# Full-array and tiled products of a step gathered into one row each, in the first pass of an attention kernel

## The chip, the cores and the metric

The kernel runs on one core of a Trainium2 chip. The core has a matrix engine (TensorE, PE in the profile; its weight loads are PEld), VectorE (DVE), ScalarE (ACT) and GpSimd (POOL), and sixteen DMA engines that move data between HBM and the on-chip memory. The engines run side by side, each through its own queue in order, and wait for each other by semaphores. The metric is the device time of one execution in microseconds, the median of several runs. Before the change it is 4040.75 us (3 runs, 4040.39 to 4041.5).

## The reference: what is computed

The input x is 8 images of 256 channels and 64 x 64 pixels, all in fp32. Two layers follow each other. Cut to what matters:

```python
# layer 0: attention of every pixel to 256 reduced keys, 8 heads of 32 channels
xr = conv(x, w_sr, stride 4)                    # 16 x 16 = 256 tokens
xr = layernorm over channels(xr) * norm_g + norm_b
q  = w_q @ x;  k, v = split(w_kv @ xr)
out = softmax(q k^T * 32**-0.5) v               # for each head
x  = x + gamma_s * (w_out @ out)
# layer 1: linear attention over two scales
qkv = w_qkv @ x                                 # 768 channels
agg = grouped 1x1 (w_pw) of depthwise 5x5 (w_dw) of qkv
... linear attention with relu, projection w_proj, batch norm, added to x
```

The change concerns layer 0 and the product qkv of layer 1, which the kernel computes together.

## The kernel before

The kernel has three passes (`first_pass`, `second_pass`, `third_pass`), and a general version that is run only where the softmax sums of the first pass leave a safe range. Only `first_pass` is changed. It does layer 0 and the qkv product.

The work is cut into steps. `order` lists them: for each image b, each of 8 strips s of 512 pixels, each half c of the heads (4 heads, 128 channels) and each half kc of the 256 keys. That makes 32 steps an image and 256 in all; n is the number of a step, and odd n are those with kc = 1. The loop runs 16 steps further to finish what is behind.

What a step asks of TensorE comes in two kinds. Products of the **full array** have 128 rows and 128 columns of weights: `queries` (q, L759), the qkv products (L885), the output products of `added` (o, L840), the stride convolution (sr, L687) and the small products of `keys_values`. Products in **tiles** use 32 rows or 32 columns of the array, so that four heads run at once: `scores` (sc, L774, four row tiles), `valued` (av, L793, four column tiles) and `counted` (den, L809, four column tiles). A matmul in fp32 shows as two records in the trace.

The chain of a step: `scores` puts four heads' scores into four of five PSUM banks (tag "mm", which the full-array products share); ScalarE turns them into exponentials e (L780). One step later, as m = n - 1, `valued` multiplies them with the values into av. At the end of an odd step `joined` (L804) lets GpSimd add the exponentials of both halves of the keys, in place, in the tiles of the even step; so these adds wait for the av that still reads these tiles. `counted` in the next even step multiplies the sums with ones, which gives the softmax denominators den. `normed` copies av (ScalarE) and divides: VectorE transposes den (L819), takes reciprocals (L820), transposes back (L822) and multiplies (L824). The result att waits two steps for `added`.

The qkv product of a pair of strips is made from 21 full-array products (`qkv`, seven for each of three pairs). They are spread over the seven steps after a pair of strips is done: `todo[n]` holds the products of step n, 2, 3, 4, 1, 4, 3 and 4 of them for n mod 8 = 3, 4, 5, 6, 7, 0 and 1, none for n mod 8 = 2. Output products come in the steps with n mod 4 = 2. For the next image, `keys_values` runs ahead in the steps with n mod 32 from 12 to 25: the stride convolution first, small products after it.

The loop body sets the order on each engine. In an odd step TensorE's row is: scores, the qkv products, valued. In an even step: scores, valued, the qkv products, queries, counted, then output products (n mod 4 = 2) and keys work where there is any. Tile, the framework, may depart from this: it orders each engine's instructions when the kernel is built, by when it believes their inputs ready, and by the written order among those that are ready. `tc.keep_in_program_order` ties one instruction behind everything written before it on its engine.

Of the kernel before, what the change touches and what calls it, by code (L numbers as in the profile page):

```python
# [574 lines left out]
def first_pass(ctx: ExitStack, tc: tile.TileContext, a, fine, planes, x2d, kd, vd, wtd):  # L575
    nc = tc.nc
# [23 lines left out]
    def load_x(b):  # L600
        x_tiles[b] = xpools[b % 2].tile([P, 2, HW], F32, tag="x", name=f"x_{b}")
        for s in range(NG):
            load_strip(b, s)
# [42 lines left out]
    def border(b):  # L646
        v = vd[b].rearrange("n y x e -> y x n e")
        src = nil.rearrange("p (n e) -> p n e", n=8)
        for i in (0, NB2 + 1):
            nc.sync.dma_start(v[i], src)  # L650
            nc.sync.dma_start(v[1 : NB2 + 1, i], src[:NB2])
# [104 lines left out]
    def queries(b, s, c):  # L756
        ps = bank(f"q_{b}_{s}_{c}")
        for ci in range(2):
            nc.tensor.matmul(  # L759
                ps,  # L760
                consts["wq"][:, ci, c * P : (c + 1) * P],
                x_tiles[b][:, ci, s * QB : (s + 1) * QB],
                start=(ci == 0),
                stop=(ci == 1),
            )
        qs = two.tile([P, QB], F32, tag="q", name=f"q_{b}_{s}_{c}")
        nc.scalar.copy(qs, ps)
        return qs

    def scores(b, s, c, kc, qs):  # L770
        scs = [bank(f"sc_{b}_{s}_{c}_{kc}_{h}") for h in range(4)]
        for h in range(4):
            rows = slice(h * D0, (h + 1) * D0)
            nc.tensor.matmul(  # L774
                scs[h], kks[b][rows, c, kc * P : (kc + 1) * P], qs[rows], start=True, stop=True
            )
        es = []
        for h in range(4):
            e = two.tile([P, QB], F32, tag="e", name=f"e_{b}_{s}_{c}_{kc}_{h}", bufs=E_BUFS)
            nc.scalar.activation(e, scs[h], AF.Exp, scale=D0**-0.5)  # L780
            es.append(e)
        return es
# [5 lines left out]
    def valued(b, s, c, kc, es):  # L788
        if kc == 0:
            sums["av"] = psum_early.tile([P, QB], F32, tag="av", name=f"av_{b}_{s}_{c}")  # L790
        for h in range(4):
            cols = slice(h * D0, (h + 1) * D0)
            nc.tensor.matmul(  # L793
                sums["av"][cols],
                vvs[b][:, kc, c * P + h * D0 : c * P + (h + 1) * D0],
                es[h],
                start=(kc == 0),
                stop=(kc == 1),
            )


    def joined(es0, es1):
        for h in range(4):
            nc.gpsimd.tensor_tensor(es0[h], es0[h], es1[h], ALU.add)  # L804

    def counted(b, s, c, es):
        sums["den"] = psum_early.tile([P, QB], F32, tag="den", name=f"den_{b}_{s}_{c}")
        for h in range(4):
            nc.tensor.matmul(sums["den"][h * D0 : (h + 1) * D0], ones_w, es[h], start=True, stop=True)  # L809

    def normed(b, s, c):
        av, den = sums["av"], sums["den"]
        i = 2 * ((b * NG + s) * 2 + c)
        att = rest.tile([P, QB], F32, tag="att", name=f"att_{b}_{s}_{c}", bufs=4)
        turn = rest.tile([P, NB, D0], F32, tag="rden", name=f"rden_{b}_{s}_{c}", bufs=1)
        one = two.tile([P, NB], F32, tag="one", name=f"one_{b}_{s}_{c}")
        nc.scalar.copy(att, av)

        nc.vector.transpose(turn.rearrange("p n d -> p (n d)"), den)  # L819
        nc.vector.reciprocal(one, turn[:, :, 0])  # L820
        r = rest.tile([P, NB, D0], F32, tag="rall", name=f"rall_{b}_{s}_{c}", bufs=1)
        nc.vector.transpose(r, one.unsqueeze(2).to_broadcast([P, NB, D0]))  # L822
        r = r.rearrange("p n d -> p (n d)")
        nc.vector.tensor_mul(att, att, r)  # L824

        def noted():
            for k, t in enumerate((turn[:, :, 0], one)):
                copy = two.tile([P, NB], F32, tag="copy", name=f"copy_{b}_{s}_{c}_{k}")
                tc.keep_in_program_order(
                    nc.scalar.activation(copy, t, AF.Copy, accum_out=seen[:, i + k : i + k + 1])  # L830
                )

        late.append(noted)
        return att

    def added(b, s, att, oc):
        xt, cols = x_tiles[b], slice(s * QB, (s + 1) * QB)
        ps = bank(f"o_{b}_{s}_{oc}")
        for c in range(2):
            nc.tensor.matmul(ps, consts["wout"][:, c, oc * P : (oc + 1) * P], att[c], start=(c == 0), stop=(c == 1))  # L840
        nc.vector.scalar_tensor_tensor(  # L841
            xt[:, oc, cols], ps, consts["gam"][:, 0:1], xt[:, oc, cols], ALU.mult, ALU.add
        )
        nc.sync.dma_start(x2d[b][oc * P : (oc + 1) * P, cols], xt[:, oc, cols])
# [5 lines left out]
    def differences(b, g):  # L850
        xt = x_tiles[b]
        x = xt[:, :, 2 * g * QB : 2 * (g + 1) * QB].rearrange("p c (h n) -> p c h n", h=2)
        b11, b12, b21, b22 = (x[:, c, h] for c in range(2) for h in range(2))
        t = halves.tile([P, 4, QB], F32, tag="differences", name=f"differences_{b}_{g}", bufs=1)
        t1, t2, t3, t4 = (t[:, i] for i in range(4))
        nc.vector.tensor_sub(t1, b12, b11)
        nc.vector.tensor_sub(t2, b22, t1)
        nc.gpsimd.tensor_tensor(t3, b22, b12, ALU.subtract)
        nc.vector.tensor_sub(t4, t2, b21)
        quarters[b, g] = b11, b21, b22, t1, t2, t3, t4  # L860
# [130 lines left out]
    order = [(b, s, c, kc) for b in range(B) for s in range(NG) for c in range(2) for kc in range(2)]  # L991
    q, es, att = {0: first}, {}, {}
    ahead = iter(())

    def qkv_lazy(b, g, pair):
        made = []

        def go(i):
            def run():
                if i == 0:  # L1000
                    made.extend(qkv(b, g, pair))
                made[i]()

            return run

        return [go(i) for i in range(7)]

    n_all = len(order)
    todo = {}
    for n in range(n_all + 16):  # L1010
        m = n - 1
        if n < n_all:
            b, s, c, kc = order[n]
            es[n] = scores(b, s, c, kc, q[n // 2])
        was, late[:] = list(late), []
        for f in was:
            f()


        if n % 2:  # L1020
            for f in todo.pop(n, ()):
                f()
        if 0 <= m < n_all:
            valued(*order[m], es[m])
        for f in todo.pop(n, ()):
            f()
        if n < n_all and kc == 0 and n + 2 < n_all:
            q.pop(n // 2 - 1, None)
            q[n // 2 + 1] = queries(*order[n + 2][:3])
        if 0 <= m < n_all and order[m][3] == 1:  # L1030
            counted(*order[m][:3], es.pop(m - 1))
            es.pop(m)
            att[order[m][:3]] = normed(*order[m][:3])
        if n < n_all and kc == 1:
            joined(es[n - 1], es[n])
        if n >= 6 and (n - 6) % 4 == 0 and (n - 6) // 4 < B * NG:
            b, s = (n - 6) // 4 // NG, (n - 6) // 4 % NG
            for oc in range(2):
                added(b, s, [att[b, s, 0], att[b, s, 1]], oc)
            if s % 2:  # L1040
                differences(b, s // 2)
                products = [p for pair in (1, 2, 0) for p in qkv_lazy(b, s // 2, pair)]
                for i, count in enumerate((2, 3, 4, 1, 4, 3, 4)):
                    todo[n + 1 + i] = products[:count]
                    products = products[count:]
        next(weights, None)
        if n < n_all:
            b, at = n // 32, n % 32
            if at == 2:
                border(b)  # L1050
            if b + 1 < B:
                if at == 10 and b > 0:
                    load_x(b + 1)
                if at == 12:
                    ahead = keys_values(b + 1)
                if 12 <= at < 20:
                    next(ahead)
                    next(ahead)
                elif at >= 20:
                    next(ahead, None)  # L1060
# [545 lines left out]
def kernel_body(ctx: ExitStack, tc: tile.TileContext, a, out):  # L1606
# [19 lines left out]
    wtd = [scratch(f"wt_{j}", [P, 16, 6 * P]) for j in range(4)]  # L1626

    first_pass(tc, a, fine, planes, x2d, kd, vd, wtd)
    second_pass(tc, a, planes, kd, vd, wtd, kvd, attd)
    third_pass(tc, a, planes, x2d, kvd, attd, out)  # L1630
# [118 lines left out]
```

## Time and profile before

The profile is one execution; its span is 4041.7 us. The first pass ends at about 2133 us, where the check of the softmax sums (L1070) runs.

| engine | busy us of 4041.7 | busy us of one image of the first pass (825 to 1082 us) |
|---|---|---|
| TensorE | 3954.6 (98%) | 256.2 of 257 |
| VectorE | 2250.5 (56%) | 141.5 |
| ScalarE | 1511.8 (37%) | 105.9 |
| GpSimd | 1275.2 (32%) | 93.2 |

| group in the first pass | count | mean ns of one |
|---|---|---|
| L774 sc, 32 rows, 512 columns streamed | 2048 | 642 |
| L793 av, 32 columns of weights, 512 streamed | 2048 | 610 |
| L809 den, the same form | 1024 | 605 |
| L759 q, full array, 512 streamed | 512 | 601 |
| L804 GpSimd add of two 128 x 512 tiles | 512 | 1315 |

A mean duration of a matmul holds its way through the array, so that records overlap; what a product costs is read from the distance between starts in the timeline. A line of the timeline gives the start and the length of a run of like instructions, in microseconds, with the idle time ahead of it and what ended that, in square brackets.

### The profile page before, as it was taken

The numbers are of one execution on the slowest core, as the hardware profiler recorded it, in microseconds if no ns is written. First come the engines' busy times: TensorE is split into PE (matmuls) and PEld (weight loads), VectorE is DVE, ScalarE is ACT, GpSimd is POOL, SyncE is SP. The second block draws the span as 40 slices with busy tenths as digits, with TensorE's granted clock in tenths as the row PEclk, the third lists the DMA queues.
The fourth block names the chain that finished last, engine by engine and source line by source line (L and its number), as shares of the span: only waits on it lengthen the run. The fifth ranks groups of instructions, "written<-read, shape, count | busy, mean of one in ns | idle before, by whom it ended". The sixth has DMA issues, their size and how long they took to land. (4 is left out here: it accounts for less than half of the span.)

```text
span 4041.7 us, 70298 instructions
## 1 busy us (share of the span) xinstructions
PE 3954.6 (98%) x27074; PEld 2260.2 (56%) x27074; DVE 2250.5 (56%) x3752; ACT 1511.8 (37%) x3473; POOL 1275.2 (32%) x1394
## 2 busy tenths in 40 slices
PE   8999999999999999999997999999999998999999
PEld 4333433434334343343335888888888886556555
DVE  2576465564655645555664566666666664444443
ACT  2334344343443434434432222222222223555444
POOL 2334233343343433424433344444444440000000
PEclk9999999999999999999998999999999998999999
DMA  7655444435344353434548878778778756767674
GB/s 236 186 172 144 143 105 145 103 98 155 93 141 112 96 157 93 134 105 107 137 111 237 247 223 235 221 219 236 222 219 233 208 167 173 229 197 235 196 235 138
DMA packets 569897, 691.37 MB, mean 171 GB/s; under 512 B 60112, under 2 KB 429264, under 8 KB 565328
## 3 DMA queue, kind: packets, MB, share of 16 engines
q1 hardware_dynamic: 569552, 686.78, 60.0%
q8 instruction: 215, 3.52, 0.4%
q14 instruction: 130, 1.06, 0.1%
HBM read 412.54 MB, written 274.10 MB: 170 GB/s over the span
## 5 line engine op out<-in xcount | busy, mean ns | idle before, releaser
L804 POOL TENSOR_TENSOR e<-e,e 128x512 f32<-128x512 f32 x512 | 656.2, 1315 | 867.0 <-PE av L793 867.0
L780 ACT ACTIVATE e<-sc 128x512 f32<-128x512 f32 x1024 | 530.6, 602 | 939.1 <-PE sc L774 939.1
L1205 PE MATMUL cv<-w,c 128*128 128x128 f32 x3072 | 386.5, 280 | 9.7 <-POOL c L1149 9.7
L1205 PEld LDWEIGHTS cv<-w,c 128*128 128x128 f32 x3072 | 361.1, 193 | 40.6 <-issue 30.3
L774 PE MATMUL sc<-q,kk 32*128 32x512 f32 x2048 | 312.9, 642 | 11.7 <-DVE x L841 5.3
L1572 DVE TENSOR_TENSOR y<-z,xs 128x256 f32<-128x256 f32 x256 | 142.6, 644 | 316.3 <-ACT z L1563 291.0
L1247 PE MATMUL sums<-vq,r 128*32 128x288 f32 x4096 | 308.3, 414 | 0.0
L885 PE MATMUL qkv<-differences,combined 128*128 128x512 f32 x576 | 306.4, 623 | 1.9 <-DVE whole L901 1.0
L819 DVE STREAM_TRANSPOSE rden<-den 128x512 f32<-128x512 f32 x128 | 91.7, 716 | 369.6 <-PE den L809 369.5
L793 PE MATMUL av<-e,vv 128*32 128x512 f32 x2048 | 275.2, 610 | 0.0
L1221 ACT ACTIVATE r<-s 128x512 f32<-128x512 f32 x256 | 160.5, 627 | 293.5 <-DVE s L1220 289.9
L1209 PE MATMUL cv<-c,w 128*128 128x128 f32 x2048 | 253.4, 277 | 0.0
L1554 PE MATMUL p<-att,wproj 128*128 128x512 f32 x512 | 249.9, 610 | 1.9 <-ACT att L1537 1.9
L1563 ACT ACTIVATE z<-p,bn 128x256 f32<-128x256 f32 x256 | 133.8, 578 | 314.8 <-PE p L1554 241.3
L687 PE MATMUL sr<-x,wsr 128*128 128x256 f32 x1024 | 238.3, 387 | 7.7 <-DMA wsr<-in_w_sr_dram 7.7
L759 PE MATMUL q<-x,wq 128*128 128x512 f32 x512 | 245.3, 601 | 0.2 <-DVE whole L901 0.2
L1554 PE MATMUL p<-agg,wproj 128*128 128x512 f32 x512 | 242.3, 596 | 0.0
L1212 ACT COPY both<-cv 128x512 f32<-128x512 f32 x128 | 75.0, 586 | 444.3 <-PE cv L1205 386.8
L1209 PEld LDWEIGHTS cv<-c,w 128*128 128x128 f32 x2048 | 239.7, 192 | 0.0
L840 PE MATMUL o<-att,wout 128*128 128x512 f32 x512 | 237.7, 605 | 0.0
L687 PEld LDWEIGHTS sr<-x,wsr 128*128 128x128 f32 x1024 | 193.2, 192 | 73.8 <-issue 40.8
L1220 DVE TENSOR_TENSOR s<-cv,both 128x512 f32<-128x512 f32 x256 | 172.1, 673 | 87.6 <-PE cv L1209 43.5
(143 smaller groups left out, 6123.4 us busy)
## 6 DMA issues: line engine op xcount, KB each, us to landing
vq<-v SPq DMA_DIRECT2D x256, 384.0 KB
planes<-stage SPq DMA_DIRECT2D x128, 578.0 KB
d<-planes SPq DMA_DIRECT2D x128, 578.0 KB
raw<-planes SPq DMA_DIRECT2D x128, 272.0 KB
x<-in_xp_dram SPq DMA_DIRECT2D x64, 512.0 KB
wsr<-in_w_sr_dram SPq DMA_DIRECT2D x128, 256.0 KB
x<-x SPq DMA_DIRECT2D x128, 256.0 KB
k<-turned SPq DMA_DIRECT2D x256, 128.0 KB
```

The costliest lines, as they stand in the source:

```text
L687: nc.tensor.matmul(ps[:, oc], w[:, ci, oc * P : (oc + 1) * P], xt[:, ci, f * NK : (f + 1) * NK], start=(f == ci == oc == 0), stop=(f == R ...
L759: nc.tensor.matmul(ps, consts["wq"][:, ci, c * P : (c + 1) * P], x_tiles[b][:, ci, s * QB : (s + 1) * QB], start=(ci == 0), stop=(ci == 1),)
L774: nc.tensor.matmul(scs[h], kks[b][rows, c, kc * P : (kc + 1) * P], qs[rows], start=True, stop=True)
L780: nc.scalar.activation(e, scs[h], AF.Exp, scale=D0**-0.5)
L793: nc.tensor.matmul(sums["av"][cols], vvs[b][:, kc, c * P + h * D0 : c * P + (h + 1) * D0], es[h], start=(kc == 0), stop=(kc == 1),)
L804: nc.gpsimd.tensor_tensor(es0[h], es0[h], es1[h], ALU.add)
L840: nc.tensor.matmul(ps, consts["wout"][:, c, oc * P : (oc + 1) * P], att[c], start=(c == 0), stop=(c == 1))
L885: nc.tensor.matmul(ps, w, x, start=True, stop=True)
L1205: nc.tensor.matmul(out, x, m, start=(da == 0), stop=(da == 1))
L1209: nc.tensor.matmul(out, m, x, start=(da == 0), stop=(da == 1))
L1247: nc.tensor.matmul(ps[h * D0 : (h + 1) * D0, : 36 * D1].rearrange("p (r n e) -> p r n e", r=3, e=D1), kt[:, par, h, 2 * r + c], vq[:, r : ...
L1554: nc.tensor.matmul(ps.rearrange("p (f q n) -> p f q n", f=4, q=4), wproj[:, j, oc * P : (oc + 1) * P], src, start=(j == 0), stop=(j == 3),)
```

## The change

Three edits. The denominators (`counted`) are computed directly behind `valued`, ahead of the step's qkv products and queries, so that the two products in column tiles follow each other. In odd steps the qkv products keep their place ahead of `valued` only where `last` holds; in the steps with keys work (n mod 32 from 12 to 25) they move behind `valued`, next to that work. VectorE's first transpose of den is tied to its place in the written order. The purpose is that the products of the full array of a step stand in one row and those in tiles in another, so that the array changes its tiling less often. The amount of arithmetic is the same.

```diff
@@ normed
-        nc.vector.transpose(turn.rearrange("p n d -> p (n d)"), den)
+        tc.keep_in_program_order(nc.vector.transpose(turn.rearrange("p n d -> p (n d)"), den))
@@ the loop of first_pass
-        if n % 2:
+        last = n < n_all and kc == 1 and not 12 <= n % 32 <= 25
+        if last:
             for f in todo.pop(n, ()):
                 f()
         if 0 <= m < n_all:
             valued(*order[m], es[m])
+            if order[m][3] == 1:
+                counted(*order[m][:3], es.pop(m - 1))
+                es.pop(m)
         for f in todo.pop(n, ()):
             f()
         if n < n_all and kc == 0 and n + 2 < n_all:
             q.pop(n // 2 - 1, None)
             q[n // 2 + 1] = queries(*order[n + 2][:3])
         if 0 <= m < n_all and order[m][3] == 1:
-            counted(*order[m][:3], es.pop(m - 1))
-            es.pop(m)
             att[order[m][:3]] = normed(*order[m][:3])
```

## The prediction

> **What bounds the kernel now.** I read the page's list of engines first, then the windows of the steady stretch of the first pass, then the waits of that pass, then the timeline of TensorE and of GpSimd over single steps.
>
> ```profile
> PE 3954.6 (98%) x27074; PEld 2260.2 (56%) x27074; DVE 2250.5 (56%) x3752; ACT 1511.8 (37%) x3473; POOL 1275.2 (32%) x1394
> ```
> ```profile
> 825.00:1082.00 257.00, 256.16 (x1100) 100.13 (x1096) 141.49 (x216) 105.88 (x258) 93.15 (x101) 1.00 0.44 119
> ```
>
> TensorE sets the end. From about 300 us the first pass repeats every 257.2 us, one image of 32 steps, with TensorE busy for 256.2 us of 257 at the full clock, VectorE for 141, ScalarE for 106, GpSimd for 93. So whatever the change takes from TensorE's row, or makes TensorE wait for, goes straight into the total. The second and third pass are not touched.
>
> The timeline of TensorE shows step n=130 (130 mod 32 = 2) between its neighbours. A line is a run of matmuls of one kind with its start and length; an fp32 product is two matmuls.
>
> ```profile
> 1108.44 1.02 PE L885 MATMUL qkv<-differences,combined 128*128 128x512 f32 x2
> 1109.30 1.02 PE L885 MATMUL qkv<-x,combined 128*128 128x512 f32 x2
> 1110.25 1.06 PE L793 MATMUL av<-e,vv 128*32 128x512 f32 x8
> 1111.25 1.14 PE L774 MATMUL sc<-q,kk 32*128 32x512 f32 x8
> 1112.32 1.07 PE L793 MATMUL av<-e,vv 128*32 128x512 f32 x8
> 1113.32 1.98 PE L759 MATMUL q<-x,wq 128*128 128x512 f32 x4
> 1115.23 1.06 PE L809 MATMUL den<-e,ones_w 128*32 128x512 f32 x6
> 1116.45 1.04 PE L809 MATMUL den<-e,ones_w 128*32 128x512 f32 x2 [0.17 <-POOL e L804]
> 1117.43 3.70 PE L840 MATMUL o<-att,wout 128*128 128x512 f32 x8
> 1121.06 1.14 PE L774 MATMUL sc<-q,kk 32*128 32x512 f32 x8
> ```
>
> Two things are to be seen. First, the price of a change of kind. Starts differ by 0.86 us per full-array product inside a run (1108.44 to 1109.30), but the last product of the run takes 0.95 (1109.30 to 1110.25), and a run's first product 0.96 as well (1106.62 to 1107.58 in the same view). A full-array run of k matmuls therefore takes 0.429k + 0.20 us: eight output matmuls 3.63. A run of av or den takes 1.00. Second, den does not run freely here: it starts at 1115.23 and the next run starts only at 1117.43, 2.20 us later instead of 1.00, because the last head waits for GpSimd.
>
> The timeline of GpSimd says why.
>
> ```profile
> 1111.45 4.96 POOL L804 TENSOR_TENSOR e<-e,e 128x512 f32<-128x512 f32 x4 [8.28 <-PE av L793]
> ```
>
> The four adds of `joined` (L804) write into the exponentials of the even step, which av of that step (L793, starting at 1110.25) still reads. So they start 1.20 us after that av starts, take 4.96, and end 6.16 after it; the last head's den follows at 1116.45, and den is over at 1117.43: **7.18 us after the start of av**. That number is fixed by GpSimd. In steps with more products ahead of den (n mod 8 = 0 or 4) den comes later anyway and doesn't wait; with one qkv product (n mod 8 = 6) it waits for 0.36.
>
> **What the Trainium skill says.** "TensorEngine Tiling (Array Packing)", Key Properties: changing the tiling mode drains TensorE, tiles within a mode run in parallel. The trace agrees: 0.20 us a full-array run. "PSUM — Partial Sum Buffer", Engine vs sequencer instructions: matmuls start and complete in program order, only weight loads are pulled ahead. So a den that waits holds every product queued behind it; above, the output products start only once den is over. "GPSIMD Engine Reference", Elementwise: a two-operand add costs about 2.6 cycles per element on GpSimd, bound by its read port; the trace has 1273 ns (median) for 512 elements, so the 5 us are not slack to be squeezed.
>
> **The change, part by part.**
>
> (1) *Odd steps with n mod 32 from 13 to 25*: the qkv products move behind av, next to the stride convolution or the small products of keys_values that end the step. Two full-array runs become one: 0.20 less. That is six odd steps an image, since in n mod 32 = 17 the convolution's products stand in step 18 in the trace: -1.2 us.
>
> (2) *den directly behind av in even steps.* Both are column tiles. The tail of the first pass shows such a pair: av x16 at 2093.03, next run at 2094.88, so 1.85 instead of 2.00, 0.15 saved. Where output products or keys work follow den, the products on both sides of it also join: a further 0.20.
>
> (3) *What den now waits for.* For an even step after an odd step of the old order (n mod 32 = 0, 2, 4, 6, 8, 10, 12, 28, 30; nine an image), take t as the start of the odd step's av. sc follows at t+1.00, av at t+2.07, den at t+2.95, free of waits it would end by t+3.9. But it can't end before t+7.18: **3.3 us of wait, with qkv, queries and output queued behind it.** Before, these products filled that time. New end of the step: 7.18 + 0.20 + 0.429 per matmul.
> - n mod 8 = 0 or 4 (five steps; 10 matmuls): 11.67 after t instead of 8.6 (t=1124.17 to 1132.81 in the same view): +3.07, together +15.4.
> - n mod 8 = 2 (two steps; queries and output, 12): 12.53 instead of 10.81: +1.72, together +3.4.
> - n mod 8 = 6 (two; 14): 13.39 instead of 10.83: +2.56, together +5.1.
> Sum 23.9, less 0.2 where convolution products join (n mod 32 = 12): **+23.7 an image**.
>
> (4) *Even steps n mod 32 = 14 to 26* follow an odd step in which av now stands ahead of 1.9 to 3.6 us of qkv products, most with 3.5 of keys work besides. den comes at t+6.6 or later: no wait. Six of them save 0.36, one 0.16, and n mod 32 = 18 loses its wait of 1.2: -3.5.
>
> (5) *Pinning the transpose of den* (L819) behind the step's VectorE work: att is used two steps later, VectorE is busy for 55%. Nothing; and the earlier den cannot be overwritten before its transpose is done, two steps on.
>
> (6) *Banks*: av and den have their own; scores after a full-array run find the last two of five banks being emptied, 0.7 us each, while q's product (1.7 us) still runs. Nothing to 0.3 us in a few steps.
>
> Net 23.7 - 1.2 - 3.5 = +19.0 an image. Six images: +114. The last has no keys work and by the same sums gets +20. The first has a slow start, where TensorE waits for other things: between 0 and 19, I take +12. The tail step n=256 has den behind the paired av: +3. Sum **+149**: 4041 + 149 = 4190.
>
> **Does the written order hold?** Tile, the framework, orders each engine's instructions at build time by when it believes inputs ready; it may put a ready product ahead of a den that it believes late. In the trace of before it kept den where it is written in all 128 places, though output products were ready and den waited on the chip. It believes the adds quicker than they are. The tightest place is n=254, with one qkv product between av and den:
>
> ```profile
> 2079.57 1.06 PE L793 MATMUL av<-e,vv 128*32 128x512 f32 x8
> 2080.57 1.12 PE L885 MATMUL qkv<-differences,combined 128*128 128x512 f32 x2
> 2081.62 1.92 PE L809 MATMUL den<-e,ones_w 128*32 128x512 f32 x6
> 2083.72 1.04 PE L809 MATMUL den<-e,ones_w 128*32 128x512 f32 x2 [0.18 <-POOL e L804]
> 2084.70 3.70 PE L840 MATMUL o<-att,wout 128*128 128x512 f32 x8
> ```
>
> So to Tile's belief the adds are done one product after av. It could still move one product ahead of some heads' den, hardly three.
>
> **The rivals.**
> - *Forecast, the wait in full*: 4190. For it: the fixed 7.18, seen in each of the steps with few products. Chance 0.50.
> - *Part of the products moved ahead*: one product fills 0.86 us of the wait and costs 0.2 to 0.3 for a further change of kind: 0.57 × 9 steps × 8 images = 41 less, 4150. Two products ahead (or both of queries) leave about +6 an image: 4090. Chance 0.27, 4120 as its middle.
> - *Faster*: Tile puts den behind all the products in the nine steps, which then stay as before, and only (1) and (4) remain: 8 × 4.7 = 37 us less, 4004. For it: the pin of part (5) makes sense where den is early, and something kept the old order in just these odd steps. Against it: n=254. Chance 0.20.
> - *No change*: parts cancel, 4040. It needs gains of 19 an image to meet the losses by accident: 0.03.
>
> **How the numbers follow.** The likeliest is 4190. Low is 4090, two products ahead; high 4212 adds the first image's full 19, 0.3 us of banks in 40 steps (12) and a few us for unseen waits. It leaves out the faster case, about 0.2, and 0.03 between. Slower by over 0.2%: 0.50 + 0.27 = 0.77; same 0.03; faster 0.20.
>
> **What would show it.** The period of an image grows from 257 to about 276 us. In step n=130 TensorE's row reads av, sc, av, den, q and o, and den's first matmul starts some 3 us after the first av, its last run's end 7.2 after. GpSimd's wait for av stays; den shows waits for POOL e in nine steps an image. Runs of full-array products get fewer: in n mod 32 = 13 to 25 no step has two. The prediction is wrong if den in steps n mod 8 = 0 and 4 stands behind the queries, or if the adds no longer start 1.20 after av.

## The result and the profile after

The changed kernel takes **4185.76 us** (median of 4 runs, 4185.57 to 4188.87), the kernel before 4040.57 in the same comparison: ratio **1.0362**, 95% interval 1.0344 to 1.038, slower by 145 us. The forecast was 4190, slower.

The page's line of engines, beside the one shown of before:

```profile
PE 4076.3 (97%) x27074; PEld 2308.3 (55%) x27074; DVE 2240.3 (54%) x3752; ACT 1516.2 (36%) x3473; POOL 1271.5 (30%) x1394
```

The instruction count of every engine is what it was. TensorE is "busy" for 122 us more although no product was added. The group of den says where, first before, then after:

```profile
L809 PE MATMUL den<-e,ones_w 128*32 128x512 f32 x1024 | 176.5, 605 | 4.8 <-POOL e L804 4.7
```
```profile
L809 PE MATMUL den<-e,ones_w 128*32 128x512 f32 x1024 | 332.7, 605 | 36.4 <-POOL e L804 34.3
```

The first figure behind the bar is the time in which at least one den was on record, the second the mean of one in ns, the third the idle time ahead of den. The busy time grows by 156 us though the mean of one is still 605 ns: heads that start 1.2 us apart, each with records of about 0.6 us, fill much of the time between them. So the wait hides in the busy share, and only 34 us show as idle time that is put down to GpSimd. It is read from starts. The timeline of TensorE at n=130, the step shown of before:

```profile
1172.47 1.07 PE L793 MATMUL av<-e,vv 128*32 128x512 f32 x8
1173.46 1.14 PE L774 MATMUL sc<-q,kk 32*128 32x512 f32 x8
1174.54 1.07 PE L793 MATMUL av<-e,vv 128*32 128x512 f32 x8
1175.42 1.84 PE L809 MATMUL den<-e,ones_w 128*32 128x512 f32 x4
1177.44 1.04 PE L809 MATMUL den<-e,ones_w 128*32 128x512 f32 x2 [0.18 <-POOL e L804]
1178.66 1.04 PE L809 MATMUL den<-e,ones_w 128*32 128x512 f32 x2 [0.17 <-POOL e L804]
1179.64 1.98 PE L759 MATMUL q<-x,wq 128*128 128x512 f32 x4
1181.46 3.60 PE L840 MATMUL o<-att,wout 128*128 128x512 f32 x8
1184.98 1.14 PE L774 MATMUL sc<-q,kk 32*128 32x512 f32 x8
```

Three things are to be seen. The order is the written one, den is not moved. av and den now touch: av's eight matmuls to den's first take 0.88 instead of 1.00. And the distance from den's first matmul (1175.42) to the queries (1179.64) is 4.22 us, where a den without a wait takes 0.97. From the first av (1172.47) to the end of den it is 7.17 us, as before; the queries, which used to run inside this time, now come after it. The step ends 12.51 after the first av instead of 10.81.

GpSimd's adds stand where they stood, 1.19 after av's start:

```profile
1173.66 4.95 POOL L804 TENSOR_TENSOR e<-e,e 128x512 f32<-128x512 f32 x4 [11.41 <-PE av L793]
```

From the windows, a steady image:

```profile
1157.00:1434.00 277.00, 273.57 (x1096) 106.82 (x1096) 140.61 (x216) 106.58 (x258) 92.65 (x101) 1.00 0.40 111
```

From the scores of one image's first step to those of the next, a steady image takes 277.4 to 277.6 us instead of 257.1 to 257.4, at the same granted clock (1.00 in both windows). The first image takes 268.3 instead of 267.9, the second 19.6 more, the next five 20.1 to 20.5 more each, the last 21.1 more.

### The profile page after: what moved, and what is told of

The parts are those of the page before. It is cut to its first block, busy times and chain, and to the rows that moved or that the text cites. A ratio compares the mean times of both kernels' runs of the same rounds, so it can differ in the third digit from the quotient of the medians.

```text
span 4187.1 us, 70247 instructions
## 1 busy us (share of the span) xinstructions
PE 4076.3 (97%) x27074; PEld 2308.3 (55%) x27074; DVE 2240.3 (54%) x3752; ACT 1516.2 (36%) x3473; POOL 1271.5 (30%) x1394
## 5 line engine op out<-in xcount | busy, mean ns | idle before, releaser
L809 PE MATMUL den<-e,ones_w 128*32 128x512 f32 x1024 | 332.7, 605 | 36.4 <-POOL e L804 34.3
L774 PE MATMUL sc<-q,kk 32*128 32x512 f32 x2048 | 321.9, 640 | 4.4 <-DVE part L967 2.7
L767 ACT COPY q<-q 128x512 f32<-128x512 f32 x128 | 75.0, 586 | 457.2 <-PE q L759 457.2
L901 DVE TENSOR_TENSOR whole<-part,qkv 128x512 f32<-128x512 f32 x256 | 175.3, 687 | 121.7 <-PE qkv L885 66.4
```

The lines of the kernel that those rows point to most:

```text
L774: nc.tensor.matmul(scs[h], kks[b][rows, c, kc * P : (kc + 1) * P], qs[rows], start=True, stop=True)
```

## The experiments

Ratios are to the kernel before, measured on the same chip in the same comparison (its median there 4036.8 to 4037.7); the changed kernel stands at 1.0362. Theory: den waits for GpSimd's adds. Rival: the row itself costs, because scores and VectorE's work stand right behind the full-array products.

| run | us | ratio, 95% interval |
|---|---|---|
| e1 own sums | 4032.98 | 0.9993 (0.9984 to 1.0002) |
| e2 den moved in seven steps only | 4019.68 | 0.9953 (0.9936 to 0.9969) |
| e3 products behind av in all odd steps | 4038.74 | 1.0002 (0.9994 to 1.0011) |
| e4 no pin | 4182.18 | 1.0361 (1.0342 to 1.0379) |
| e5 half the adds | 4036.64 | 0.9998 (0.9989 to 1.0007) |
| e6 den a step later | 3997.28 | 0.9906 (0.9887 to 0.9925) |
| e7 before, own sums | 4034.25 | 0.9996 (0.9987 to 1.0005) |
| e8 den in its old place | 4031.61 | 0.9988 (0.9981 to 0.9994) |
| e9 den a step later, tuned | 3976.54 | 0.9849 (0.9834 to 0.9863) |
| e10 before, less room | 4034.59 | 0.9993 (0.9985 to 1.0002) |

**e5, half the adds: the dose.**

```diff
-            nc.gpsimd.tensor_tensor(es0[h], es0[h], es1[h], ALU.add)
+            nc.gpsimd.tensor_tensor(es0[h][:, : QB // 2], es0[h][:, : QB // 2], es1[h][:, : QB // 2], ALU.add)
```

> The changed kernel with GpSimd adding only the first 256 of 512 columns of each pair of exponentials (the sums of the other half are left out, so the denominators of half the pixels lack one half of the keys). Nothing else moves. Theory: an add takes about 0.65 us instead of 1.27, the four end 3.7 us after av's start instead of 6.16, the wait of den falls from 3.3 to about 0.8 us: 22 us less an image in nine steps, 4020 to 4035 us in all. Rival (GpSimd is not what den waits for): 4185 us.

The timelines of GpSimd and TensorE in the step n=128, first of the changed kernel, then of e5:

```profile
1157.28 4.97 POOL L804 TENSOR_TENSOR e<-e,e 128x512 f32<-128x512 f32 x4 [6.68 <-PE av L793]
```
```profile
1159.04 1.86 PE L809 MATMUL den<-e,ones_w 128*32 128x512 f32 x4
1161.08 1.04 PE L809 MATMUL den<-e,ones_w 128*32 128x512 f32 x2 [0.19 <-POOL e L804]
1162.30 1.04 PE L809 MATMUL den<-e,ones_w 128*32 128x512 f32 x2 [0.17 <-POOL e L804]
1163.28 1.98 PE L885 MATMUL qkv<-x,wqkv 128*128 128x512 f32 x4
```
```profile
1089.78 2.80 POOL L804 TENSOR_TENSOR e<-e,e 128x256 f32<-128x256 f32 x4 [4.32 <-PE av L793]
```
```profile
1091.54 2.14 PE L809 MATMUL den<-e,ones_w 128*32 128x512 f32 x8
1093.61 1.98 PE L885 MATMUL qkv<-x,wqkv 128*128 128x512 f32 x4
```

The four adds take 2.80 us instead of 4.97, and from den's first matmul to the next product it is 2.07 us instead of 4.24: 2.17 us less add, 2.17 us less wait. An image takes 258.2 us, 19.3 less than after, or 2.15 for each of the nine steps. TensorE's row is the same in order and content. So GpSimd's adds are the cause of the loss: two thirds of den's wait went with them here, and in six of the nine steps of e1, below, all of it. An add of 256 columns takes 0.70 us and not the 0.65 expected, which in nine steps and eight images is 14 us and more than accounts for the 2 us by which the time lies above the range.

**e1, the adds started earlier.**

```diff
-            nc.gpsimd.tensor_tensor(es0[h], es0[h], es1[h], ALU.add)
+            nc.gpsimd.tensor_tensor(both[h], es0[h], es1[h], ALU.add)   # tiles of their own
...
-            joined(es[n - 1], es[n])
+            es[n - 1] = joined(es[n - 1], es[n])
```

> The order of the changed kernel, but GpSimd writes the sums of the exponentials into tiles of their own and not in place, so the adds need not wait for av (room for them: 11 instead of 12 tiles of exponentials, 4 instead of 6 of whole). Theory (den waits 3.3 us for adds that start 1.2 us after av): the adds now start when the odd step's exponentials are done, some 1.9 us after its scores start, and end 4.96 later; den is then free of waits where four qkv products precede av, and waits about 0.9 us in three steps an image where two do. 27 us less an image, 3985 to 4000 us in all, below the kernel before. Rival (the loss comes from the row itself: scores and VectorE work now stand right behind the full-array products and the transpose is pinned): hardly better than 4185, above 4150.

4033 us: the direction of the theory and against the rival, but 33 us above the range. Six of the nine dens are free or nearly so (0.97 us, in a few places up to 1.5); three, where two products precede av, still take 3.3. GpSimd's timeline there:

```profile
858.05 1.78 POOL L863 TENSOR_TENSOR differences<-x 128x512 f32<-128x512 f32 x1 [8.05 <-DVE x L846]
859.79 2.95 POOL L806 TENSOR_TENSOR esum<-e,e 128x512 f32<-128x512 f32 x2
862.68 0.15 POOL L869 MEMSET stage<- 128x68 f32 x1
862.89 0.22 POOL L870 MEMSET stage<- 128x68 f32 x1
863.01 2.50 POOL L806 TENSOR_TENSOR esum<-e,e 128x512 f32<-128x512 f32 x2
```

The adds are in GpSimd's queue behind `differences` for the pair of strips just ended, and two memsets split them: they end at 865.51, 7.2 us after ScalarE begins the step's exponentials (858.34). Taking one wait away let another part of GpSimd's row show. Three waits of 2.3 instead of the expected 0.9 make 4.2 us an image, 34 in all, which is most of the miss: an image takes 256.1 us, 21.4 less than after, where 27 less was expected.

**e2, e8, e3 and e4: the parts.** e2 keeps den in its old place in the nine steps of part (3):

```diff
-            if order[m][3] == 1:
+            if order[m][3] == 1 and 12 <= m % 32 <= 25:
                 counted(*order[m][:3], es.pop(m - 1))
...
+            if not 12 <= m % 32 <= 25:
+                counted(*order[m][:3], es.pop(m - 1))
```

> den directly behind av only in the even steps n mod 32 = 14 to 26, whose odd step has av ahead of the qkv products; in the other even steps den stands behind products and queries as before. The edit of the odd steps and the pin stay. Theory: the whole loss sits in the nine steps taken back, and what remains is the gain of 4.7 us an image less the new 1.2 us wait of the scores in n mod 32 = 24: 4005 to 4015 us. Rival (odd steps, pin or banks cost): above 4050.

4019.7, faster than before by 0.5%. The steady image takes 253.7 to 255.0. The whole loss sits in the nine steps. What the others gain is 17 us between the medians, and the time lies 5 us above the range.

e8 puts den back everywhere (`counted` again just ahead of `normed`):

> The changed kernel with den back behind products and queries in all even steps; left of the change are the odd steps n mod 32 = 13 to 25 (products behind av) and the pin. Theory: 0.2 us in six odd steps an image, and the 1.2 us wait of den in n mod 32 = 18 goes: 2.4 us an image gained, up to 1.2 lost in the scores: 4020 to 4035 us. Rival (these two edits are what costs): well above 4060 us.

4031.6, as expected, a gain of 0.12%: the odd steps and the pin are not what costs. Between e8 and e2 lie 12 us for the earlier den in seven steps.

e3 sets `last = False`:

> The qkv products behind av in all odd steps. The adds then run beside the products: den of the next even step comes 6.6 us after av where there are four products, with next to no wait, and 4.9 us after it where there are two, with a wait of about 1.3 us (three steps an image). Against it, the next scores stand right behind the products and wait up to 1 us for banks. Theory: 21 to 25 us less an image, 4000 to 4040 us. Rival (the row costs, not the adds): more waits of the scores, 4185 us or more.

4038.7, at the upper end of what was expected. den is free (0.97) behind four products. Behind two it takes 3.0 to 3.2, a wait of 2.0 to 2.2 instead of the 1.3 expected: as in e1, GpSimd's `differences` and memsets stand ahead of and between these adds, which in n=99 end 7.2 us after av's start instead of 6.16. In return scores take 0.57 longer in n mod 32 = 0, 2, 8 and 10. Moving the products to the other side of av gives the adds their time, and part of it is lost in these scores; that they wait for banks was expected and not tested.

e4 leaves the pin out:

> The changed kernel without tying VectorE's transpose of den to the written order. Theory: the pin is worth nothing either way while den waits: 4175 to 4195 us. Rival (the pin delays VectorE work that empties the banks): clearly less, toward 4100 us, and no wait of the scores in n mod 32 = 24.

4182.2, ratio 1.0361: the pin is worth nothing that shows, and the 1.2 us wait of scores in n mod 32 = 24 is there without it too.

**e6, den later instead of earlier.** den is placed behind av of the next odd step; ScalarE's copy of av stays.

```diff
+        if 0 <= m - 1 < n_all and order[m - 1][3] == 1:
+            counted(*order[m - 1][:3], es.pop(m - 2))
+            es.pop(m - 1)
+            att[order[m - 1][:3]] = normed(*order[m - 1][:3])
...
         if 0 <= m < n_all and order[m][3] == 1:
-            att[order[m][:3]] = normed(*order[m][:3])
+            taken(*order[m][:3])        # ScalarE's copy of av into att
```

> den moves one step further back instead of forward: into the next odd step, directly behind its av; ScalarE's copy of av stays in the even step. The adds then have a whole step more. Theory: no wait of den in any step, one full-array run in each even step, av and den together: against the kernel before 4.3 us an image of den's waits, 16 times 0.15 and about 11 times 0.2 us for changes of tiling, and 1.2 us in odd steps, 10 us an image: 3955 to 3975 us. Rival (changes of tiling cost nothing that can be had back, or att comes too late for the output products): 4000 to 4060 us.

3997.3, 0.9% faster than before: den stands behind av, each even step has its full-array products in one row, and in the steady images den has no wait in any step (0.97). It misses the range by 22 us. Scores that stand right behind the full-array products wait: in the last image, which has no keys work, six of them by 0.6 to 2.3 us, and in the others in n mod 32 = 22, 24 and 26 by 0.4, 1.8 and 0.5.

**e9, the same with those products ahead of av.**

```diff
-        last = n < n_all and kc == 1 and not 12 <= n % 32 <= 25
+        last = n < n_all and kc == 1 and not (12 <= n % 32 <= 20 and n < n_all - 32)
```

> den in the next odd step as in the run before, and the qkv products ahead of av in all odd steps but n mod 32 = 13 to 19 of the first seven images, where stride convolution stands between them and the next scores. The trace of the run before shows scores waiting behind the products for banks: in sum about 11 us in the last image, and 0.4, 1.8 and 0.5 us in three steps of each other image. Theory: these waits go, less three changes of tiling of 0.2 us an image: 20 to 27 us less than with den late alone, 3970 to 3985 us. Rival (VectorE is late by itself, and the wait moves to another product): 3990 to 4000 us.

**3976.5, ratio 0.9849**, as expected, and the fastest version of the study. Its timelines of TensorE (n=128 with the start of n=129, then the end of n=129) and of GpSimd:

```profile
1068.18 1.14 PE L774 MATMUL sc<-q,kk 32*128 32x512 f32 x8
1069.25 1.06 PE L793 MATMUL av<-e,vv 128*32 128x512 f32 x8
1070.24 1.99 PE L887 MATMUL qkv<-x,wqkv 128*128 128x512 f32 x4
1072.06 1.02 PE L887 MATMUL qkv<-differences,combined 128*128 128x512 f32 x2
1072.92 1.88 PE L759 MATMUL q<-x,wq 128*128 128x512 f32 x4
1074.73 1.22 PE L774 MATMUL sc<-q,kk 32*128 32x512 f32 x8
```
```profile
1079.51 1.07 PE L793 MATMUL av<-e,vv 128*32 128x512 f32 x8
1080.40 1.04 PE L809 MATMUL den<-e,ones_w 128*32 128x512 f32 x8
1081.37 1.14 PE L774 MATMUL sc<-q,kk 32*128 32x512 f32 x8
```
```profile
1067.52 5.42 POOL L804 TENSOR_TENSOR e<-e,e 128x512 f32<-128x512 f32 x4
```

The even step is scores, av and one full-array run, and GpSimd's adds (1067.52 to 1072.94) lie beside it; the den that needs them comes behind the av of the next odd step. A steady image takes 247.7 to 248.8 us, 8.9 less than before on the mean. Not all of this is the price of changes of kind: 4.3 us are the waits that den had in the old order (1.2 in n mod 32 = 2, 10 and 18, 0.36 in 6 and 30), which are gone because the adds now have a whole step. And a part of the scores' waits may only have moved: in n mod 32 = 23 the qkv products take 4.3 to 4.7 us in most images, instead of 3.63.

**e7 and e10: what moving the adds costs.** e7 gives the old order sums of their own; e10 takes only the room that this needed (`E_BUFS` 11, four tiles of `whole`).

> The kernel before in its old order, with the sums in tiles of their own (and the same room made as in the run of the changed order). Theory: only the waits that den has in the old order go, 1.2 us in three steps and 0.36 us in two of an image: 34 us in all, 4000 to 4015 us. Less room for exponentials may cost a little. If own tiles alone gain far more, the adds' place was not the cause there. Rival: 4040 us.

> The kernel before with only the room taken that the own sums needed: 11 tiles of exponentials instead of 12 and 4 tiles of whole instead of 6. If the new 0.6 us waits of the scores in the old order with own sums come from the lack of room, this run shows them too and takes 4055 to 4065 us; if they come from VectorE's product att being held up while GpSimd adds, it takes 4035 to 4045 us with scores of 1.07 us in n mod 32 = 2, 6 and 10.

e7 took 4034 where 4000 to 4015 was expected, no gain that can be told from none. (The profiled run, at 4024 the fastest of twelve, shows an image 1.6 us shorter than before; the twelve together don't show it.) In the steps n mod 32 = 2, 6, 10 and 30, den has lost its wait (1.00 instead of 2.20 and 1.36), but scores now take 1.7 instead of 1.07. e10 has scores of 1.07 and 4034.6, so the room taken costs nothing that shows. What differs is VectorE. The two groups by line, between 300 and 2040 us, first of the kernel before, then of e7:

```profile
L824 DVE TENSOR_TENSOR att<-att,rall 128x512 f32<-128x512 f32 x110 | 76.1, 692 | 9.6
```
```profile
L829 DVE TENSOR_TENSOR att<-att,rall 128x512 f32<-128x512 f32 x110 | 112.3, 1021 | 9.5
```

This product reads two operands in on-chip memory. In e7 the 44 of its 128 that run beside a GpSimd add take 1.60 us on the mean, the 84 others 0.70. One takes 1.71, from 846.81 to 848.52, while GpSimd's adds run from 846.70 to 852.11; the work that empties banks comes a microsecond late, and scores start into banks that are not yet free. That chain is read from the trace; no run changed it alone. "SBUF — State Buffer", Who interferes with whom, in the Trainium skill says that a VectorE instruction with two operands in SBUF contends with a GpSimd instruction that reads SBUF, and one with at most one, outside the modes that use two ports, does not. The trace agrees: VectorE's adds into the stage, with one operand in PSUM, take 0.69 both beside GpSimd's adds and alone. The slower product need not cost time: in e9 119 of the 128 run beside an add and take 1.37 us on the mean, GpSimd's four adds take 5.42 instead of 4.96, and it is still the fastest version.

## Why the prediction was right, step by step

- *TensorE's row sets the end*: right. Every microsecond of den's wait was in the image's period.
- *7.18 us from av's start to den's end*: right, 7.16 to 7.20 in all these steps from n=34 on. The wait is 3.0 to 3.3 us; e5 shows its cause by dose.
- *The written order holds*: right for den in every step from the second image on. In the first image, at n=28, Tile put den behind three qkv products and the first half of the queries, so that the rival of products moved ahead did happen once; and in the tail step n=256 one qkv product stands ahead of the last head's den. Neither weighs in the total.
- *Part (3), +23.7 an image*: right. The nine steps take 23.8 to 23.9 us more in a steady image; n mod 8 = 2 ends at 12.51 where 12.53 was worked out.
- *Parts (1), (2) and (4), -4.7*: av and den together save 0.15, runs that join 0.20, the wait in n mod 32 = 18 is gone. Too good by 1.2: in n mod 32 = 24 scores take 2.23 instead of 1.07, right behind four products and the small product rs of keys_values. Part (6) had "nothing to 0.3" for banks, with the queries' product to cover the time; here no such product stands between. This is the mis-sized term: 20.3 an image instead of 19.0. The step n=120 of the changed kernel:

```profile
1092.08 0.61 PE L726 MATMUL rs<-ident,wide 128*128 128x128 f32 x4
1092.62 2.30 PE L774 MATMUL sc<-q,kk 32*128 32x512 f32 x8
1094.85 1.06 PE L793 MATMUL av<-e,vv 128*32 128x512 f32 x8
```

In the images with keys work the scores of this step take 2.23 or more in every run with the qkv products behind av; before and in e9, where these products stand ahead of av, they take 1.07. So the place of the products is the cause; that banks are the link was not tested.

- *The first image, +12*: it was +0.4. From start to start, den takes 18.7 us more in its 32 steps, scores and av 18.0 less: the waits that TensorE had there anyway took up the loss. The later images at 0.6 to 1.5 more and the first at 12 less nearly cancel. That the total is only 4 us off is therefore luck in part; its main term, part (3), is not.
- *Part (5), the pin*: right, nothing, by e4.
- *The faster rival* (den behind the products in the nine steps) did not happen in the changed kernel, but e2 is its order: 4019.7, where 4004 had been worked out. Most of what an image lacks of the 4.7 us (it gains 2.9) are again the scores of n mod 32 = 24, which take 2.23 there too.

## What to carry to other kernels

Before products are gathered by kind, look up for each one which engine makes its input and when that ends. Here saving 0.15 to 0.36 us of tiling changes in a step took away the work that hid 3.3 us of another engine's adds. Moved the other way, behind those adds, den could be gathered with av and the kernel gained 1.5%, about half of it from waits that den had before. And a wait between matmuls that start one by one shows only in part as idle time: count from start to start.

## What was not expected of the hardware

den's wait of some 3.3 us a step is booked for the most part as busy time of TensorE: 332.7 us of den after and 176.5 before, with the mean of one unchanged at 605 ns, while the idle time ahead of den only grows from 4.8 to 36.4. And VectorE's product of two on-chip operands grows from 0.70 to 1.60 us beside GpSimd's adds; where the adds run therefore matters to VectorE also, whether it costs time, as read in e7, or not, as in e9.
